# A graph-attention layer on one core: the first group takes h W before the softmax, its attention runs on quarters of the array, and transfers are put in order of use

## The chip, the core and the metric

The kernel runs on one core of a Trainium2 chip. The core has a matrix engine (TensorE, "PE" in the profile, with its weight loads as "PEld"), VectorE (DVE), ScalarE (ACT), GpSimd (POOL) and SyncE (SP), which issues most transfers. ACT and POOL issue transfers too, each from its own queue. The metric is the device time of one execution in microseconds (us); it is the median of three runs. A profiled execution of the same kernel gives the rows that are quoted.

## The reference

Everything is float32. There are 128 graphs of 64 nodes with 512 features. The graph layer has four heads.

```python
h = maximum(layernorm(x), 0)                       # x: [128, 64, 512]
Wh = einsum('bnf,hfo->bhno', h, W_heads)           # four heads, 512 x 512 each
e  = f1[:, :, :, None] + f2[:, :, None, :]         # f1 = Wh . a[:, :512], f2 = Wh . a[:, 512:]
e  = where(adj > 0, leaky_relu(e, 0.01), -1e9)
h1 = elu(einsum('bhnm,bhmo->bhno', softmax(e), Wh))  # heads side by side: [128, 64, 2048]
out = elu(one such head on h1, with W_out (2048 x 512) and a_out)
y  = relu(out @ w1 + b1) @ w2 + b2 + out
return x + layernorm(y) * gamma + beta
```

Two orders are possible for a head: softmax(e) times (h W), or (softmax(e) times h) times W. The scores f1 and f2 need neither product: f1 = h (W a1), so they can be had from h and the "folded" vectors W a1 and W a2.

## The kernel before

**Tiles and groups.** A tile t holds 128 rows, that is two graphs (NB = 2). Four tiles (G = 4) form a group; there are NG = 16 groups. The main loop goes over groups g. In the turn of g it runs `project1(g, h)` for the four heads, then `project2(g)` (the product with W_out), each beside "side" work of other groups: attention weights of later groups (`stage_a`), attention of the second layer (`stage_e(g-1)`), and the feed-forward part of group g-1 (`feed_forward`).

**Large products.** A product of a 512 x 512 block by a group's 512 columns is cut into 2 x 2 blocks and computed with seven block products in place of eight (`unit`). Block products 5, 6, 7 and 4 use sums of weight blocks, which `weight_sums(m)` makes once on GpSimd and stores in DRAM (`TC[m]`); products 1, 2 and 3 use blocks of the weight itself. `piece(m, p)` loads a block (256 KB) on SP's queue into a ring of 11 buffers. For heads 0 and 1 of group 0 the sums are still in SBUF and are used from there (`DIRECT`). Each of the seven is four float32 matmuls of 256 columns, and the profile counts two instructions for one such matmul ("x8").

**First layer of a group.** `norm1(t)` normalizes a tile (statistics on DVE, the power on POOL, the activation on ACT). `transpose_h(t)` turns it on PE, and `project_f(g)` multiplies it by `wa`, the folded vectors. `scores1(g)` sets out the sums f1 + f2, `softmax` (through `attn_weights(p)`, two tiles at a time) makes the weights A on DVE and ACT, `transpose_weights(p)` turns them. `attend1(g)` multiplies the weights with h, before W: four blocks z of all heads, copied out of PSUM by ACT and DVE. `project1(g, h)` then multiplies by W, applies elu, and leaves blocks `H1`, from which `project2(g)` works. So in every group softmax comes first and the large products after it.

**The start.** Before the main loop, the four W_heads are loaded whole on ACT's queue (`fetch`), x, adj and a_heads on SP's. The fold is done for heads 0, 1 and 3 on DVE (`fold_dve`: 8 multiply-and-accumulate instructions per head, against rows of a_heads which `spread_a` spreads over the partitions with PE), for head 2 on PE (`fold_pe`: transposes of W, then matmuls of two columns). Then come `project_f(0)`, `scores1(0)`, the softmax of both tile pairs, the turned weights, `attend1(0)` and `project1(0, 0)`. The weight sums of W_out (`more_sums`, m = 4 to 7) lie beside `project1(0, 1..3)`, behind the softmax's end.

**What sets the order.** The Tile layer puts each engine's instructions in an order by their place in the program, simulated readiness and free buffers; what follows a `high_priority` is drawn forward. Engines then run their own queues in order. A dependency added by hand keeps one instruction behind another. PSUM has six banks for large results (`bank`, tag "mm") and two for small ones (`aux`). SBUF tiles with one tag share a buffer: the W_heads of the start lie in the buffers which later hold h1's blocks (`homes`), their sums in those of the feed-forward part (`stages`).

Of the kernel before, what the change touches and what calls it, by code (L numbers as in the profile page):

```python
# [14 lines left out]
ALPHA = 0.01  # L15
# [7 lines left out]
def gat_preln_kernel(  # L23
# [27 lines left out]

    nc = tc.nc
# [27 lines left out]

    def aux(shape, name):
        return ps.tile(shape, FP, tag="aux", name=name, bufs=2)
# [16 lines left out]
    aj = const.tile([P, N], mybir.dt.int32, name="aj")  # L99
    for b in range(NB):  # L100
        nc.sync.dma_start(out=aj[ts(b, N), :], in_=adj)
# [4 lines left out]
    ah = wk.tile([2 * H * KC, P], FP, tag="elu", name="ah", bufs=3)  # L106
    nc.sync.dma_start(out=ah, in_=a_heads.rearrange("h (r p) -> (h r) p", p=P))
# [9 lines left out]
    def masks():  # L117

        nc.vector.memset(wa, 0.0)
        id32 = const.tile([P, 32], FP, name="id32")  # L120
        nc.vector.tensor_reduce(id32, ident.rearrange("p (j r) -> p r j", r=32), AX.X, ALU.add)
        nc.vector.tensor_add(headrow, id32[:, 0:H], id32[:, H:2 * H])
        nc.vector.tensor_reduce(isf, id32[:, 0:2 * H].rearrange("p (c h) -> p c h", c=2), AX.X, ALU.add)
        for q in range(2):
            par = sm.tile([P, 1], FP, tag="par", name=f"par{q}")
            nc.vector.tensor_reduce(
                par, ident.rearrange("p (a q r) -> p q a r", a=2, q=2)[:, q], AX.XY, ALU.add
            )
            nc.vector.tensor_scalar(isq[:, q], isf, par, None, ALU.mult)
# [3 lines left out]
        nc.vector.tensor_scalar(negm, aj, 0.0, None, ALU.is_gt)  # L133
        nc.vector.tensor_scalar(negm, negm, NEG, -NEG, ALU.mult, ALU.add)
        nc.vector.tensor_add(eye, ident[:, 0:N], ident[:, N:2 * N])
# [6 lines left out]
    homes = ("h11", "h22", "h12", "wh2", "out", "wh2", "out", "wh2", "out", "out")  # L142
    stages = ("ot", "rt", "out", "hS", "ot", "rt", "ot", "rt", "ot", "rt")
    MT, TC = {}, {}
    DIRECT = {}

    def fetch(m):
        MT[m] = big.tile([P, KC, O], FP, tag=homes[m], name=f"pw{m}")
        queue = nc.scalar if m < H else nc.gpsimd
        queue.dma_start(out=MT[m], in_=mats[m].rearrange("(k p) o -> p k o", p=P))  # L150

    def spread_a(m):

        ab = []
        for c in range(2):
            pb = bank(f"pab{m}_{c}").rearrange("p a b -> p (a b)")
            r = 2 * m + c
            nc.tensor.matmul(
                pb, ident[0:2 * H, r:r + 1].to_broadcast([2 * H, P]), ar, start=True, stop=True
            )  # L160
            ab.append(pb)
        return ab

    def turn_a():

        rows = H * 2 * KC
        pt = aux([P, rows], "pah")
        nc.tensor.transpose(pt, ah, ident[0:rows, 0:rows])
        aT = wk.tile([P, H, 2, KC], FP, tag="s1", name="aT")
        nc.scalar.copy(aT.rearrange("p h c o -> p (h c o)"), pt)  # L170
        return aT

    def fold_dve(m, ab):

        for k in range(KC):
            for c in range(2):
                junk = wk.tile([P, O], FP, tag="t", name=f"jk{c}_{m}_{k}")
                nc.vector.scalar_tensor_tensor(
# [4 lines left out]
    def fold_pe(m, aT):  # L183

        pw = aux([P, KC, 2], "pwa")
        for k in range(KC):
            pt = bank(f"pwt{m}_{k}").rearrange("p a b -> p (a b)").rearrange("p (o q) -> p o q", o=KC)
            for o in range(KC):
                nc.tensor.transpose(pt[:, o, :], MT[m][:, k, ts(o, P)], ident)
            wT = wk.tile([P, KC, P], FP, tag="elu", name=f"wT{m}_{k}", bufs=3)  # L190
            nc.scalar.copy(wT, pt)
            for o in range(KC):
                nc.tensor.matmul(
                    pw[:, k, :], wT[:, o, :], aT[:, m, :, o],
                    start=(k == 0 and o == 0), stop=(o == KC - 1), skip_group_check=True,
                )
        nc.scalar.copy(wa[:, :, m:m + H + 1:H], pw)

    def weight_sums(m, after=None):

        w = MT.pop(m)
        b11, b12 = w[:, 0:2, 0:Q], w[:, 0:2, Q:O]
        b21, b22 = w[:, 2:4, 0:Q], w[:, 2:4, Q:O]
        tag = stages[m]
        if tag[1] == "t":
            s = [big.tile([P, 2, 2, Q], FP, tag=f"{tag}{i}", name=f"pt{m}_{i}") for i in range(2)]
        else:
            both = big.tile([P, 2, 2, 2, Q], FP, tag=tag, name=f"pt{m}")
            s = [both[:, 0], both[:, 1]]
# [3 lines left out]
        for ins in free if after is not None else ():  # L213
            tc.add_manual_dep(
                ins.ins, after.ins.name,
                mybir.DependencyInfo(mybir.DependencyClass.Sync, mybir.DependencyReason.DATA),
                reason="the sums come behind it",
            )
# [4 lines left out]
        if m < 2:  # L223
            for p, i in ((5, 0), (6, 1), (7, 2), (4, 3)):
                DIRECT[m, p] = s[i // 2][:, i % 2]

    def piece(m, p):

        if (m, p) in DIRECT:
            return DIRECT.pop((m, p))  # L230
# [109 lines left out]
    def norm_stats(src, tag, t):  # L340
# [4 lines left out]
        if tag == "n1" and t >= 2 * G:  # L345
            tc.add_manual_dep(
                ins.ins, LAST["pe"].ins.name,
                mybir.DependencyInfo(mybir.DependencyClass.Sync, mybir.DependencyReason.DATA),
                reason="x may come late: not in front of what is urgent",
            )  # L350
# [5 lines left out]
        nc.gpsimd.tensor_tensor(rstd, ve, mhalf, ALU.pow)  # L356
        return mv[:, 0:1], rstd

    def norm1(t):
# [7 lines left out]
        if t % G >= 2:  # L367
# [14 lines left out]
    def project_f(g):  # L382


        pf = aux([P, P], f"pf{g}")
        for k in range(KC):
            for j in range(G):
                nc.tensor.matmul(
                    pf[32 * j:32 * j + 32], wa[:, k, :], HT[G * g + j][:, k, :],
                    start=(k == 0), stop=(k == KC - 1), skip_group_check=True,  # L390
                )
        L = sm.tile([P, 2, P], FP, tag="L", name=f"L{g}", bufs=1)
# [12 lines left out]
    def scores1(g):  # L405

        L, R = LR.pop(g)
        pe = [aux([P, 2, H * N], f"s1pe{g}_{a}") for a in range(2)]
        for q in range(2):
            for a in range(2):  # L410
                for b in range(NB):
                    rows, cols = slice(64 * a, 64 * a + 64), slice(b * N, (b + 1) * N)
                    nc.tensor.matmul(
                        pe[a][cols, q, :].rearrange("p (h m) -> p h m", h=H), L[rows, q, cols],
                        R[rows, :, cols], start=(q == 0), stop=True, skip_group_check=True,
                    )
        for a in range(2):
            E1[2 * g + a] = pe[a].rearrange("p t (h m) -> p (t h) m", m=N)

    def softmax(pe, f1, q, tag, t):  # L420
# [4 lines left out]
        mask = negm[:, None, :].to_broadcast([P, q, N])  # L425
        if f1 is None:
            nc.vector.tensor_tensor(e, pe, mask, ALU.add)
        else:
            nc.vector.tensor_tensor(e, pe, f1[:, :, None].to_broadcast([P, q, N]), ALU.add)
            nc.vector.tensor_tensor(e, e, mask, ALU.add)  # L430
        nc.vector.scalar_tensor_tensor(e, e, ALPHA, e, ALU.mult, ALU.max)
        mx = sm.tile([P, q], FP, tag=w + "mx", name=f"{tag}mx{t}")
        nc.vector.tensor_reduce(mx, e, AX.X, ALU.max)
        nc.vector.tensor_tensor(e, e, mx[:, :, None].to_broadcast([P, q, N]), ALU.subtract)
        nc.scalar.activation(e, e, AF.Exp)
        s = sm.tile([P, q], FP, tag=w + "s", name=f"{tag}s{t}")
        nc.vector.tensor_reduce(s, e, AX.X, ALU.add)
        r = sm.tile([P, q], FP, tag=w + "r", name=f"{tag}r{t}")
        nc.vector.reciprocal(r, s)
        if q == 8:  # L440
            A = sm.tile([P, 2, H + 1, N], FP, tag=w + "A", name=f"{tag}A{t}", bufs=1)
            nc.vector.tensor_tensor(
                A[:, :, 0:H], e.rearrange("p (t h) m -> p t h m", h=H),
                r.rearrange("p (t h) -> p t h", h=H)[:, :, :, None].to_broadcast([P, 2, H, N]), ALU.mult,
            )
            LAST["A"] = nc.vector.tensor_copy(A[:, :, H], A[:, :, 0])
# [23 lines left out]
    def transpose_weights(p):  # L470
        A = A1.pop(p)
        for j in range(2):
# [3 lines left out]
            pt = aux([P, NB * H, N], f"s1pt{t}")  # L476
            for h in range(H):
                to = pt[:, h:h + H + 2:H + 1] if h + 1 < H else pt[:, h:h + 2]
                nc.tensor.transpose(to, A[:, j, h:h + 2].rearrange("p b m -> p (b m)"), ident)  # L479
# [87 lines left out]
    def flat(ap):  # L567
        return ap.rearrange("p a b -> p (a b)")

# [3 lines left out]
    def z_sums(g, h):  # L573
        z = ZB[g]
        ZSUM[h] = new_sums(f"z{g}_{h}")
        eng = nc.vector if (g, h) == (0, 0) else nc.gpsimd
        sums(eng, z["S1"][:, h], z["11"][:, h], z["12"][:, h], z["22"][:, h], *ZSUM[h])

    def project1(g, h):
# [3 lines left out]
        first = (g, h) == (0, 0)  # L583
        if h == 0:
            for b in ("11", "12", "S1", "22"):
                tag = "hS" if b == "S1" else "h" + b
                H1[b] = big.tile([P, H, 2, T], FP, tag=tag, name=f"h{b}_{g}")
# [3 lines left out]
        def post(what, a, b=None, to=None):  # L591
# [13 lines left out]
            post, (1, 2, 6, 5, 7, 3, 4) if first else (1, 5, 6, 2, 3, 7, 4),  # L605
# [9 lines left out]
        ]  # L615

# [180 lines left out]
    masks()  # L797
    for t in range(G):
        norm1(t)
    ab = {m: spread_a(m) for m in (0, 1)}  # L800
    aT = turn_a()
    fold_dve(0, ab[0])
    fold_dve(1, ab[1])
    fold_pe(2, aT)
    for t in range(G):
        transpose_h(t)
    fold_dve(3, spread_a(3))
    for m in range(H):
        weight_sums(m, LAST["nb"])
    project_f(0)  # L810
    scores1(0)
    for p in range(2):
        attn_weights(p)
    softmax_end = LAST["A"]
    transpose_weights(0)
    attn = attend1(0)
    for fn in attn[:2]:
        fn()
    head0 = project1(0, 0)
    for fn in head0[:2]:  # L820
        fn()
    transpose_weights(1)
    for fn in attn[2:]:
        fn()
    z_sums(0, 0)
# [14 lines left out]
    def more_sums(m):  # L840
        fetch(m)
        weight_sums(m, softmax_end)

    for t in range(G, 2 * G):
        prefetch(t)
    for g in range(NG):
        if g >= 1:
            side = stage_e(g - 1)
        else:
            side = sum(stage_a(1), [])  # L850
            for i, m in ((5, 4), (9, 5), (12, 6), (17, 7)):
                side.insert(i, lambda m=m: more_sums(m))
        done, n = 0, 6 * H
        for i in range(n):
            if i % 6 == 0:
                steps = head0 if (g, i) == (0, 0) else project1(g, i // 6)
            if (g, i // 2) != (0, 0):
                steps[i % 6]()
            while done * n < (i + 1) * len(side):
# [64 lines left out]
```

## Time and profile before

The three timed runs took 2317.66, 2319.98 and 2321.33 us. The profiled execution has a span of 2318.7 us.

| engine | busy us | share of the span |
|---|---|---|
| PE | 2279.8 | 98% |
| PE weight loads | 1922.7 | 83% |
| DVE | 1272.2 | 55% |
| POOL | 1029.9 | 44% |
| ACT | 905.5 | 39% |

The start by stretches, busy us of each engine:

| stretch, us | PE | DVE | ACT | POOL | transfers, GB/s |
|---|---|---|---|---|---|
| 0 to 60 | 41.38 | 36.37 | 17.32 | 34.84 | 294 |
| 60 to 115 | 54.24 | 35.77 | 30.50 | 38.82 | 168 |
| 115 to 230 | 111.69 | 51.73 | 46.47 | 62.02 | 186 |
| 230 to 370 | 140.00 | 78.34 | 55.90 | 60.41 | 155 |

A row of a group of instructions gives line, engine, operation, the tile written and those read, the shape, and the count. A row of a timeline begins with start and length in us; several alike are merged, and brackets hold the idle time before and what ended it. A row of a wait reads: who waited for whom, then the sum in us, how often, and the longest. A row of a window holds, after its bounds and length, an engine's busy time with its count of instructions, then the clock granted to PE (1.00 is full), the share of transfers and their rate. Matmuls are pipelined: the time from start to start is what one costs, and the length of one is longer.

### The profile page before, as it was taken

The numbers are of one execution on the slowest core, as the hardware profiler recorded it, in microseconds if no ns is written. First come the engines' busy times: TensorE is split into PE (matmuls) and PEld (weight loads), VectorE is DVE, ScalarE is ACT, GpSimd is POOL, SyncE is SP. The second block draws the span as 40 slices with busy tenths as digits, with TensorE's granted clock in tenths as the row PEclk, the third lists the DMA queues.
The fourth block names the chain that finished last, engine by engine and source line by source line (L and its number), as shares of the span: only waits on it lengthen the run. The fifth ranks groups of instructions, "written<-read, shape, count | busy, mean of one in ns | idle before, by whom it ended". The sixth has DMA issues, their size and how long they took to land. (4 is left out here: it accounts for less than half of the span.)

```text
span 2318.7 us, 33446 instructions
## 1 busy us (share of the span) xinstructions
PE 2279.8 (98%) x11933; PEld 1922.7 (83%) x11933; DVE 1272.2 (55%) x2210; ACT 905.5 (39%) x1623; POOL 1029.9 (44%) x917
## 2 busy tenths in 40 slices
PE   6999999999999999999999999999999999999997
PEld 4878888888888888888888888888888888888885
DVE  6635465555646555465555646555464654744427
ACT  2534425153352534425254252533525244251512
POOL 6664544425344352444425444253443525533324
PEclk8999999999999999999999999999999999999999
DMA  8545464554545445454454545445453454635543
GB/s 296 174 171 195 133 183 135 157 161 133 183 135 176 131 147 178 133 182 132 151 171 133 182 135 162 150 140 182 132 179 131 147 180 128 182 119 168 163 146 104
DMA packets 259571, 366.40 MB, mean 158 GB/s; under 512 B 24232, under 2 KB 147144, under 8 KB 259408
## 3 DMA queue, kind: packets, MB, share of 16 engines
q1 hardware_dynamic: 252784, 343.31, 47.3%
q0 software_dynamic: 4512, 16.78, 2.0%
q10 hardware_dynamic: 2112, 4.19, 0.5%
q8 instruction: 96, 1.57, 0.3%
q14 instruction: 67, 0.55, 0.1%
HBM read 336.92 MB, written 27.26 MB: 157 GB/s over the span
## 5 line engine op out<-in xcount | busy, mean ns | idle before, releaser
L322 PE MATMUL g_b<-w,h 128*128 128x256 f32 x2560 | 592.5, 379 | 0.0
L322 PEld LDWEIGHTS g_b<-w,h 128*128 128x128 f32 x2560 | 481.4, 190 | 63.7 <-issue 0.9
L307 PE MATMUL g_a<-z,w 128*128 128x256 f32 x1520 | 360.9, 380 | 0.7 <-DVE g_a L597 0.7
L307 PE MATMUL g_a<-zs_z,w 128*128 128x256 f32 x1504 | 350.9, 381 | 0.0
L307 PEld LDWEIGHTS g_a<-zs_z,w 128*128 128x128 f32 x1504 | 282.0, 190 | 60.8 <-issue 24.3
L307 PEld LDWEIGHTS g_a<-z,w 128*128 128x128 f32 x1520 | 287.2, 190 | 45.0 <-DVE g_a L597 6.1
L601 POOL TENSOR_TENSOR hS<-hS,h 128x512 f32<-128x512 f32 x64 | 83.1, 1299 | 354.8 <-DVE hS L565 354.8
L322 PE MATMUL g_b<-w,hS 128*128 128x256 f32 x1024 | 238.5, 379 | 0.0
L563 ACT ACTIVATE exc<-g_a 128x512 f32<-128x512 f32 x256 | 152.1, 594 | 179.0 <-DVE g_a L597 106.7
L565 DVE SCALAR_TENSOR_TENSOR h<-exc,g_a 128x512 f32<-128x512 f32 x192 | 131.7, 686 | 157.3 <-ACT exc L564 156.2
L322 PEld LDWEIGHTS g_b<-w,hS 128*128 128x128 f32 x1024 | 192.1, 190 | 25.8 <-issue 1.0
L564 ACT ACTIVATE exc<-exc 128x512 f32<-128x512 f32 x256 | 161.5, 631 | 7.0
L631 POOL TENSOR_TENSOR h<-h,h 128x512 f32<-128x512 f32 x64 | 86.8, 1364 | 135.3 <-PE g_b L322 135.3
L631 POOL TENSOR_TENSOR h<-hS,h 128x512 f32<-128x512 f32 x64 | 81.2, 1270 | 142.5 <-PE g_b L322 142.5
L481 ACT COPY at<-s1pt 128x512 f32<-128x512 f32 x64 | 34.7, 588 | 279.8 <-PE s1pt L479 279.8
L332 POOL TENSOR_TENSOR zs_z<-zS,z 128x512 f32<-128x512 f32 x63 | 89.0, 1414 | 122.6 <-PE g_a L307 118.6
L773 POOL TENSOR_TENSOR xr<-xr,bs 128x512 f32<-128x512 f32 x64 | 96.1, 1502 | 72.6 <-DMA xr<-in_x_dram 58.4
L307 PE MATMUL g_c<-ot,w 128*128 128x256 f32 x512 | 122.8, 383 | 1.4 <-DVE ot L735 1.4
L322 PE MATMUL g_d<-w,rt 128*128 128x256 f32 x512 | 121.5, 380 | 2.2 <-DVE o L765 1.5
L307 PE MATMUL g_a<-zS,w 128*128 128x256 f32 x496 | 117.2, 379 | 0.0
L655 DVE SCALAR_TENSOR_TENSOR jf<-wh,ao 128x512 f32<-128x512 f32 x128 | 99.0, 811 | 31.8 <-ACT wh L637 31.6
L333 POOL TENSOR_TENSOR zs_z<-z,zs_z 128x512 f32<-128x512 f32 x63 | 85.1, 1351 | 61.8 <-PE g_a L307 39.1
(159 smaller groups left out, 3485.8 us busy)
## 6 DMA issues: line engine op xcount, KB each, us to landing
w<-tc SPq DMA_DIRECT2D x632, 256.0 KB, 2.7
w<-in_L_gnn_W_heads_dram SPq DMA_DIRECT2D x192, 256.0 KB, 3.0
w<-in_L_gnn_W_out_dram SPq DMA_DIRECT2D x192, 256.0 KB, 2.7
w<-in_L_gnn_w_dram SPq DMA_DIRECT2D x96, 256.0 KB, 2.7
x<-in_x_dram SPq DMA_DIRECT2D x64, 256.0 KB, 3.8
xr<-in_x_dram SPq DMA_DIRECT2D x128, 128.0 KB, 2.7
out_dram<-o SPq DMA_DIRECT2D x128, 128.0 KB, 2.4
tc<-pt POOLq DMA_DIRECT2D x20, 512.0 KB, 4.2
```

Source lines behind the costliest of these rows:

```text
L307: LAST["pe"] = nc.tensor.matmul(bk[:, o, :], w[:, k, ts(o, P)], a[:, k, :], start=start and o == 0 and k == 0, stop=k == 1, skip_group_che ...
L322: LAST["pe"] = nc.tensor.matmul(bk[:, j, :], a[:, k, ts(j, P)], w[:, k, :], start=start and k == 0 and j == 0, stop=i == len(ms) - 1 and k ...
L332: eng.tensor_tensor(s2, s1, a11, ALU.subtract)
L333: eng.tensor_tensor(s4, a12, s2, ALU.subtract)
L481: nc.scalar.copy(AT[t].rearrange("p b h n -> p (b h) n"), pt)
L563: nc.scalar.activation(ex, src, AF.Relu, scale=-1.0)
L564: nc.scalar.activation(ex, ex, AF.Exp, scale=-1.0)
L565: nc.vector.scalar_tensor_tensor(dst, ex, -1.0, src, ALU.add, ALU.max)
L601: nc.gpsimd.tensor_tensor(dst, dst, H1["22"][:, h], ALU.add)
L631: nc.gpsimd.tensor_tensor(dst[:, h], x0[:, h], x1[:, h], ALU.subtract)
L655: nc.vector.scalar_tensor_tensor(junk, WH2[g][:, j], 1.0, ao[:, c, :], ALU.mult, ALU.mult, accum_out=f[:, c, j:j + 1],)
L773: nc.gpsimd.tensor_tensor(xr, xr, bs, ALU.add)
```

## The change

Only group 0 is computed in another way. Its four heads take h W first (`head_w(m, j)`: tile j by head m, four matmuls of 512 columns, the copy by ACT into `HW`). The scores are folded beside it, all four heads on DVE (`fold`); `fold_pe` and `turn_a` go. `attend0(h, r)` then multiplies the turned weights with `HW`, four matmuls of 64 rows and 64 columns of the array for each pair of tiles, and applies elu to the result in its natural layout; `turn0(h, r)` transposes that on PE and copies it into `H1`. `attend1(0)` and `project1(0, h)` are no longer called.

The transfers are put in order: only W of head 0 stays on ACT's queue, heads 1 to 3 go to SP's behind x, adj goes to POOL's, a_heads comes second on SP's, and its other layout `ah` goes. The loads of W_out for `weight_sums` come during the head products, each held behind one of them. The weight sums are all kept in the buffers "ot" and "rt", and `DIRECT` goes, as does `HNS` of group 0. Group 1's transposes and `project_f` lie among group 0's attention, its `scores1`, softmax and turned weights at the beginning of `project2(0)`.

```diff
     X[0] = load(0)
-    aj = const.tile([P, N], mybir.dt.int32, name="aj")
-    for b in range(NB):
-        nc.sync.dma_start(out=aj[ts(b, N), :], in_=adj)
     ar = wk.tile([2 * H, O], FP, tag="elu", name="ar", bufs=3)
...
-    homes = ("h11", "h22", "h12", "wh2", "out", "wh2", "out", "wh2", "out", "out")
+    homes = ("h11", "h22", "h12", "wh2", "out", "hS", "out", "hS", "out", "out")
...
-        queue = nc.scalar if m < H else nc.gpsimd
+        queue = nc.scalar if m == 0 else nc.sync if m < H else nc.gpsimd
...
-        if tag == "n1" and t >= 2 * G:
+        if tag == "n1" and t >= G:
+            behind(ins, LAST["pe"], "x may come late: not in front of what is urgent")
...
-        pf = aux([P, P], f"pf{g}")
+        pf = aux([P, P], f"pf{g}") if g else flat(bank("pf0"))[:, 0:P]
...
+                if g == 0 and k == 0:
+                    behind(ins, LAST["pe"], "the fold is not done sooner")
...
+    def head_w(m, j):
+        pb = aux([P, O], f"hw{m}_{j}")
+        for k in range(KC):
+            LAST["pe"] = LAST["hw", m, j] = nc.tensor.matmul(
+                pb, HT[j][:, k, :], MT[m][:, k, :], start=k == 0, stop=k == KC - 1
+            )
+        nc.scalar.copy(flat(HW[j][:, m]), pb)
+
+    def attend0(h, r):
+        pa = [flat(bank(f"pu{h}_{r}_{b}")) for b in range(NB)]
+        for b in range(NB):
+            rows = slice(b * N, (b + 1) * N)
+            for c in range(2):
+                nc.tensor.matmul(
+                    pa[b][c * N:(c + 1) * N], AT[2 * r + c][rows, b, h, :],
+                    flat(HW[2 * r + c][rows, h]), start=True, stop=True, skip_group_check=True,
+                )
+        for b in range(NB):
+            ex = wk.tile([P, O], FP, tag="elu", name=f"ex0{h}_{r}_{b}", bufs=3)
+            if b == 0:
+                nc.scalar.activation(ex, pa[b], AF.Relu, scale=-1.0)
+                nc.scalar.activation(ex, ex, AF.Exp, scale=-1.0)
+            else:
+                nc.vector.tensor_scalar(ex, pa[b], 0.0, None, ALU.min)
+                nc.scalar.activation(ex, ex, AF.Exp)
+            NAT[h, r, b] = wk.tile([P, O], FP, tag=f"zs{2 + b}", name=f"nat{h}_{r}_{b}")
+            nc.vector.scalar_tensor_tensor(NAT[h, r, b], ex, -1.0, pa[b], ALU.add, ALU.max)
+
+    def turn0(h, r):
+        for b in range(NB):
+            nat = NAT.pop((h, r, b))
+            pt = flat(bank(f"ptu{h}_{r}_{b}")).rearrange("p (c q) -> p c q", c=KC)
+            for c in range(KC):
+                nc.tensor.transpose(pt[:, c, :], nat[:, ts(c, P)], ident)
...
+        if r == 1:
+            nc.gpsimd.tensor_tensor(H1["S1"][:, h], H1["S1"][:, h], H1["22"][:, h], ALU.add)
...
+    for m in range(3):
+        fold(m, ab[m])
+    for j in range(G):
+        transpose_h(j)
+        head_w(0, j)
+    weight_sums(0, LAST["nb"])
+    fold(3, spread_a(3))
+    masks()
+    weight_sums(1, LAST["nb"])
+    for j in range(3):
+        head_w(1, j)
+
+    def more_sums(m):
+        fetch(m, LAST["hw", *{4: (0, 1), 5: (0, 3), 6: (1, 2), 7: (2, 1)}[m]])
+        weight_sums(m)
+
+    more_sums(4)
     project_f(0)
+    weight_sums(2, LAST["nb"])
+    head_w(1, 3)
+    more_sums(5)
+    head_w(2, 0)
     scores1(0)
...
+    transpose_weights(0)
+    head_w(3, 0)
+    attend0(0, 0)
+    attend0(1, 0)
+    head_w(3, 1)
+    transpose_weights(1)
+    turn0(0, 0)
+    attend0(2, 0)
+    head_w(3, 2)
+    turn0(1, 0)
+    attend0(0, 1)
+    head_w(3, 3)
+    turn0(2, 0)
+    attend0(1, 1)
+    turn0(0, 1)
+    attend0(3, 0)
+    turn0(1, 1)
+    attend0(2, 1)
+    for fn in scores[:2]:
+        fn()
+    turn0(3, 0)
+    attend0(3, 1)
+    project_f(1)
+    turn0(2, 1)
+    turn0(3, 1)
...
-            run(project2(g), first + early + norms + scores + turns + [
+            mixed = side1 + attn[:2] + norms[:1] + attn[2:] + norms[1:] + [nothing] * 3
+            run(project2(g), mixed + early + scores + turns + [
                 load_rows, lambda: sums_late(M1), lambda: sums_late(M2)
             ])
```

## The prediction

> **What bounds the kernel now.** I read the page first: the busy row of TensorE (PE) and the table of 40 slices.
>
> ```profile
> PE 2279.8 (98%) x11933; PEld 1922.7 (83%) x11933; DVE 1272.2 (55%) x2210; ACT 905.5 (39%) x1623; POOL 1029.9 (44%) x917
> ...
> PE   6999999999999999999999999999999999999997
> ```
>
> PE is busy in 98% of the span, and only the first and last of the 58 us slices are loose. The diff touches group 0 alone, so the other fifteen groups (140.0 us each in the windows 230 to 370 and 370 to 510) are not at stake: what can change lies before about 185 us, where group 1's first product starts. Second, the waits of PE:
>
> ```profile
> PE pab L158 <- DMA ar<-in_L_gnn_a_heads_dram: 8.2, 1, 8.2
> PE s1pt L479 <- DVE s1A L442: 5.4, 1, 5.4
> PE s1pe L413 <- DVE n1ve L354: 2.8, 1, 2.8
> PE pwt L189 <- DMA pw<-in_L_gnn_W_heads_dram: 2.1, 1, 2.1
> ```
>
> All four stand at the start: 18.5 us in which PE has nothing, because softmax precedes every large product. Third, the timeline of PE (start, length, tile, count):
>
> ```profile
> 22.55 1.09 PE L378 MATMUL pth<-ident,hn 128*128 128x128 f32 x4
> ...
> 35.41 2.15 PE L388 MATMUL pf<-hT,wa 128*32 128x128 f32 x32
> 40.37 1.99 PE L413 MATMUL s1pe<-R,L 64*64 64x256 f32 x16 [2.82 <-DVE n1ve L354]
> 47.74 1.94 PE L479 MATMUL s1pt<-ident,s1A 128*128 128x128 f32 x8 [5.38 <-DVE s1A L442]
> 49.61 6.22 PE L539 MATMUL pz<-at,hn 64*128 64x256 f32 x32
> ...
> 80.51 1.08 PE L388 MATMUL pf<-hT,wa 128*32 128x128 f32 x32
> ...
> 101.84 1.04 PE L479 MATMUL s1pt<-ident,s1A 128*128 128x128 f32 x8
> 102.71 1.89 PE L307 MATMUL g_a<-z,w 128*128 128x256 f32 x8
> ...
> 184.47 1.89 PE L307 MATMUL g_a<-z,w 128*128 128x256 f32 x8
> 186.20 1.89 PE L307 MATMUL g_a<-zS,w 128*128 128x256 f32 x8
> ...
> 218.24 1.09 PE L697 MATMUL pa<-wh,at 64*64 64x512 f32 x8
> 219.26 1.99 PE L307 MATMUL g_a<-zs_z,w 128*128 128x256 f32 x8
> ```
>
> The same 32 score matmuls take 2.15 us at 35 us and 1.08 us at 80 us, the same 8 transposes 1.94 and 1.04: PE runs at half speed until attention's matmuls have streamed for some 4 us. The windows show when it ends:
>
> ```profile
> 44.00:46.00 2.00, 0.00 (x0) 0.50 0.97 375
> ...
> 52.00:54.00 2.00, 2.00 (x13) 0.51 0.33 127
> 54.00:56.00 2.00, 2.00 (x17) 1.00 0.00 0
> ```
>
> (The third number is PE's busy time, the one after the count its clock. Before 41 us the record says 1.00, but the lengths above say one half.) So before 49.6 us no projection work is done, and group 0 is some 50 us late.
>
> [...] 17.5 to 37 us is filled mostly with transposes and two-column matmuls and stays slow. [...]
>
> **The change, part by part.** PE's prices at full clock, from start-to-start times: 8 instructions of 256 columns (four fp32 matmuls, two instructions each) 1.73 us, so one of 512 columns 0.432; 8 transposes 0.87; one attention of four quarter-array matmuls, 512 wide, 1.02 (the shape of L697); the score sets of L388 and L413 1.0 each. At half clock a 512-column instruction of spread_a took 0.853.
>
> Group 0's PE work afterwards, up to its project2:
> - head_w, 16 times four matmuls of 512 columns: 16 x 8 x 0.432 = 55.3. It replaces 28 x 1.73 = 48.4 of the seven-product form: 6.9 more, but it needs only h and W.
> - attend0 8 x 1.02 = 8.2, and turn0's 64 transposes 7.0. attend1(0), which goes, would cost 7.7 warm (as for group 1, 120 to 140 us) and took about 10.
> - transposes of h 1.75, of the weights 1.75, score sets 2.0.
> - spread_a: 12 instructions slow, 10.2, the last four fast, 1.7. The transposed fold of W2 (fold_pe: pwt 3.7 plus pwa 7.0 us busy) goes, as does aT.
> - group 1's transposes and projection of scores, still in this stretch: 2.75.
> Sum 90.7.
>
> It starts when ar lands. ar moves ahead of adj, and three of the 1 MB loads leave ACT's queue for SP's, behind x. x0 landed 2.4 us after its issue ended; with ar's issue ending near 1.8 us I take 5 us (4.2 to 8.2 as bounds). ACT is freed too: it issued loads until 12.2 us and only then normalized; now one load is some 2.9 us of issue, so h of tile 0 is there by 7 to 8, under the 10 us of spread_a. W1 to W3 are needed on PE only every 13.8 us and land by about 20 at the 300 to 365 GB/s seen, so SP's order hides. 5 + 90.7 = 95.7. head_w's first 4 to 5 us run slow: 2.5 more, 98.2.
>
> Fold, masks and softmax now lie beside head_w. DVE needs 32 folds x 0.61 = 19.5, eight tiles' statistics 8, masks 2.5, R and U 1.7, two softmaxes 10.5: 42 of the 60 us before weight transposes are wanted (my sum puts those near 66 us). The fourth head's spread comes about 32 us, its fold ends near 40, scores1 is placed near 54, softmax ends 61 and 66: hidden, with 5 us to spare. head_w's PSUM copies (0.59 us, ACT) hide under 3.46 us each, unless ACT's queue stands behind an exponential that waits for DVE; early on two small PSUM buffers serve both transposes and products. I give these handovers 2 us (0 to 5).
>
> From the first attention on ACT has, per head and half, two activations and one more exponential (3 x 0.6) and two copies (about 0.4 each): 2.6 us, 8 times 21, with head copies 2.4, weight copies 2.3 and group 1's copies 2.4: 28 us, over some 30 us of PE. After the last head_w it is about 15.5 on ACT against 12.4 on PE: 3.5 us of stall (0, if project2's first product, 6.9 us and ready by then, fills it; 8 if every chain is exposed). 98.2 + 2 + 3.5 = 103.7 for project2's start.
>
> project2(0) took 115.68 to 184.47, 68.8 us, with 63.4 of work (48.4, attend1 7.7, group 2's scores 5.5, the late g_a 1.73), so 5.4 of gaps. Now it also holds group 1's scores1 and weight transposes (2.75) and no g_a: 64.4 + 5.4 = 69.8 (gaps 3 to 10: group 1's softmax and group 2's norms come after each other, but the stage has 42 us left after attention). End 173.5 against 184.5: 11.0 us less.
>
> The edits of statistics' order, of the softmax's loop (one piece as before) and of b11/stages have no work of their own. POOL loses hns and z_sums for group 0, and the sums of W_out (four tensor operations of 1.27 and 1.1 of issue, 6.2 each) come earlier: eight sums are 50 us from about 13 us on. The waiting fetches stand in POOL's own queue, ahead of norms and S1 additions. Their waits end with head_w(0,1), (0,3), (1,2), (2,1), near 23, 34, 46 and 58 us; the last load, 7.7 us median to landing, and its sums end near 75. H1's S1 uses that load's buffer and is first written near 90: hidden.
>
> 2318.7 - 11.0 = 2307.7 for the profiled span; the timed runs' median, 2319.98, less 11 gives **2309**.
>
> **The rivals.** (a) *Better packed*: project2's first product fills the turn phase, handovers cost nothing and ar lands at 4.2: 6.3 us more, about 2302. For it: PE has nearly always ready work. Against: two small PSUM buffers. (b) *Gain eaten in attention and turn*: quarter-array attention and transposes alternate for 12.4 us without a large product. If transposes do not hold the clock, this stretch takes 12.4 more, and ACT's 3.5 then hide: 11 - 8.9 = 2 us gain, 2318. With only ACT's 8 exposed, 2313.5. For it: 17 to 37 us above. Against: attention fills half of each 2 us with the whole array. (c) *POOL becomes the bound, slower*: if each fetch of W_out is issued only behind the sums of the one before, a chain of 4 x (7.7 + 6.2) = 56 us follows about 38 us of earlier work and ends near 94; norms behind it push it further. The mechanism decides from the end of the last sum: turn0 of the second half waits for its buffer from 90 on, PSUM banks fill, and PE stops. At 101 the gain is gone; past about 106 the kernel is slower by over 0.2%; an end at 112 gives 2331. For it: POOL waited 4.4 and 10.0 us for W_out's landing at 97 and 121 us. Against: the fetches' waits end long before. (d) The head products could be done early with nothing gained if softmax came no sooner; but PE's slots are then already spent on them, so I give this no share of its own.
>
> **How the numbers follow.** Likeliest 0.52, own range 2304 to 2314. (a) 0.13. (b) 0.25, half of it within 0.2% of before. (c) 0.10. 0.2%, 4.6 us, is about what a measurement of this kernel can tell from no change. Faster (below 2315.3): 0.52 + 0.13 + 0.13 = 0.78; within: 0.12; slower: 0.10. The range runs from 2300 to 2320: it leaves out (c) and little of (a) and (b).
>
> **What would show it.** Right: pab near 5 us; head products from about 15, fast by 20; PE in the first 60 us at 54 or more of busy time instead of 41; group 1's first L307 product near 173. Wrong: PE's waits for ACT copies above 6 us in sum; transposes of turn0 at 0.21 us each instead of 0.11; turn copies released by POOL; project2(0) longer than 75 us.

## The result, and the profile after

The change made the kernel slower. Medians of four runs each, taken together: 2330.4 us (2328.9 to 2332.11) after, 2320.65 (2317.66 to 2321.39) before; the ratio is 1.0045, with a 95% interval of 1.0027 to 1.0062. The forecast was 2309, with a range of 2300 to 2320: wrong in its sign, and outside its range by 10 us. The profiled span is 2329.7 us against 2318.7, 11.0 more.

The page's busy row and PE's row of slices:

```profile
PE 2289.5 (98%) x11856; PEld 1896.2 (81%) x11856; DVE 1274.2 (55%) x2227; ACT 901.9 (39%) x1621; POOL 1014.9 (44%) x908
...
PE   8899999999999999999999999999999999999997
```

The first slice did rise, from 6 to 8: PE has its early work. But the second is an 8 where it was a 9, and PE is busy for 9.7 us more in all, with 77 instructions fewer. PE's waits say where it stands idle now, and its timeline (start, length, tile, count; idle time before and its releaser in brackets) says when:

```profile
PE hw L612 <- ACT hw L615: 7.5, 1, 7.5
PE pab L171 <- POOL n1rs L327: 5.4, 1, 5.4
PE g_a L282 <- ACT t_a L248: 4.0, 1, 4.0
PE pth L351 <- ACT hT L353: 3.2, 2, 2.6
PE s1pt L468 <- DVE s1A L426: 2.6, 2, 2.1
```

```profile
5.36 10.57 PE L171 MATMUL pab<-ar,ident 8*128 8x512 f32 x12 [5.36 <-POOL n1rs L327]
...
18.91 5.46 PE L612 MATMUL hw<-pw,hT 128*128 128x512 f32 x8
...
35.51 14.00 PE L612 MATMUL hw<-pw,hT 128*128 128x512 f32 x32 [0.73 <-ACT hT L353]
...
73.21 5.61 PE L612 MATMUL hw<-pw,hT 128*128 128x512 f32 x8 [7.53 <-ACT hw L615]
...
115.11 1.89 PE L297 MATMUL g_b<-w,h 128*128 128x256 f32 x8
...
125.50 1.43 PE L468 MATMUL s1pt<-ident,s1A 128*128 128x128 f32 x8 [2.10 <-DVE s1A L426]
...
162.22 1.82 PE L351 MATMUL pth<-ident,hn 128*128 128x128 f32 x8 [2.59 <-ACT hT L353]
...
189.35 1.89 PE L282 MATMUL g_a<-z,w 128*128 128x256 f32 x8
...
214.72 3.78 PE L282 MATMUL g_a<-zs_z,w 128*128 128x256 f32 x8 [4.05 <-ACT t_a L248]
```

The old waits for softmax at the start are gone. Two new large ones have come, at 66 and at 211 us. Both cost twice: the products at 73.21 and at 214.72 take 5.61 and 3.78 us instead of 3.60 and 1.89, at a PE clock of 0.50 in both places (72 to 76 and 214 to 220 us), where it was 1.00 before the waits. The windows around the first (the last fields are PE's busy time and count, its clock, the share of transfers and GB/s) show it fall and return:

```profile
70.00:72.00 2.00, 0.00 (x0) 0.56 0.61 177
...
74.00:76.00 2.00, 2.00 (x4) 0.50 0.65 262
...
78.00:80.00 2.00, 2.00 (x12) 1.00 0.53 122
```

So 7.53 us of idling were followed by a clock of 0.50, which was 1.00 again by 78. The prediction counted a slow clock at the start and, in rival (b), for the transposes, but behind no stall.

The difference by stages. Project2(0) starts at 115.11 where 103.7 was forecast (11.4 late), takes 74.24 us where 69.8 was (4.4), and after group 1's first product at 189.35 some 7.0 are lost again around 211 us (4.05 of wait, about 3 of half clock). Of these, 6.1 remain at the end: from that product on the span has 2140.35 us, where before had 2134.23. With the 11.0 of gain that the forecast had: -11.0 + 11.4 + 4.4 + 6.1 = 10.9, against 11.0 measured.

**What holds PE at 66 us.** The timeline of all engines:

```profile
58.94 1.27 POOL L194 TENSOR_TENSOR pt<-pw 128x512 f32<-128x512 f32 x1 [1.19 <-DMA tc<-pt]
...
66.21 1.08 POOL L327 TENSOR_TENSOR n1rs<-n1ve,mhalf 128x1 f32<-128x1 f32 x2
...
68.52 0.50 POOL L337 TENSOR_SCALAR n1nb<-n1mv,n1rs 128x1 f32<-128x1 f32 x2
68.81 0.42 DVE L323 BATCH_NORM_AGGREGATE n1mv<-n1st 128x2 f32<-128x6 f32 x2 [6.54 <-POOL n1nb L337]
68.81 1.52 ACT L339 ACTIVATE hn<-x,n1nb,n1rs 128x512 f32<-128x512 f32 x2 [10.60 <-POOL n1nb L337]
...
69.15 2.87 DVE L420 TENSOR_TENSOR s1e<-s1e,s1mx 128x512 f32<-128x512 f32 x1
...
72.05 0.63 ACT L421 ACTIVATE s1e<-s1e 128x512 f32<-128x512 f32 x1 [1.72 <-DVE s1e L420]
72.59 0.57 ACT L615 COPY hw<-hw 128x512 f32<-128x512 f32 x1
```

Read it from the last row back. The copy that PE waits for is 0.57 us of work, but ACT stands in order behind an exponential (72.05) and two normalizations (68.81). The normalizations waited 10.60 us for group 1's reciprocal deviations and the step after them (n1nb), two operations on a single column per tile, which GpSimd reached only at 66.21: from 58.94 it had the weight sums of the fourth head, with 1.19 us of waiting for its own DRAM write before them. DVE had the variances ready by 59.9. DVE itself then stood for 6.54 us: the statistics of group 1's next two tiles wait for the same n1nb, and the softmax's subtraction (69.15) stands behind them. That subtraction took 2.87 us, and the exponential waited for it; the same instruction takes 0.69 at 76.70, where GpSimd runs no tensor operation. It ends just after the first break between two of GpSimd's operations (71.46 to 71.55). By ACT's row one can divide the stall: its normalizations were over at 70.33, and 1.72 us of waiting for the subtraction followed. An estimate from this is 1.7 us for the long subtraction and the other 5.8 for the queue.

**What holds PE at 211 us** is the long DVE operation alone:

```profile
207.96 5.48 DVE L418 SCALAR_TENSOR_TENSOR s2e<-s2e 128x256 f32<-128x256 f32 x1
...
211.89 1.26 POOL L307 TENSOR_TENSOR zs_z<-zS,z 128x512 f32<-128x512 f32 x1
213.23 1.34 POOL L308 TENSOR_TENSOR zs_z<-z,zs_z 128x512 f32<-128x512 f32 x1
213.36 0.68 DVE L247 TENSOR_TENSOR g_a<-g_a,s_a 128x512 f32<-128x512 f32 x1
...
214.08 0.59 ACT L248 COPY t_a<-g_a 128x512 f32<-128x512 f32 x1 [7.73 <-DVE g_a L247]
```

An operation of group 0's second softmax lies on DVE for 5.48 us and ends just after GpSimd, in tensor operations without a break from 208.22, first has one (213.15 to 213.23); g_a's addition and PE stand behind it. What fills GpSimd's row there are sums of z and h that had been kept back by w2's weight sums, at 202.08 to 207.15. Before, w2's sums ran at 192 to 197 and this softmax at 200.6 to 207.9, its instructions on DVE taking at most 1.67 us, and the one in question:

```profile
203.02 0.41 DVE L431 SCALAR_TENSOR_TENSOR s2e<-s2e 128x256 f32<-128x256 f32 x1
```

The change moved both, and they met.

### The profile page after: what moved, and what is told of

It is laid out like the page before. It is cut to its first block, busy times and chain, and to the rows that moved or that the text cites. A ratio compares the mean times of both kernels' runs of the same rounds, so it can differ in the third digit from the quotient of the medians.

```text
span 2329.7 us, 33260 instructions
## 1 busy us (share of the span) xinstructions
PE 2289.5 (98%) x11856; PEld 1896.2 (81%) x11856; DVE 1274.2 (55%) x2227; ACT 901.9 (39%) x1621; POOL 1014.9 (44%) x908
## 5 line engine op out<-in xcount | busy, mean ns | idle before, releaser
L282 PE MATMUL g_a<-z,w 128*128 128x256 f32 x1440 | 342.8, 381 | 0.0
L282 PE MATMUL g_a<-zs_z,w 128*128 128x256 f32 x1440 | 338.0, 383 | 4.0 <-ACT t_a L248 4.0
L282 PEld LDWEIGHTS g_a<-zs_z,w 128*128 128x128 f32 x1440 | 271.0, 191 | 64.0 <-issue 24.3
L282 PEld LDWEIGHTS g_a<-z,w 128*128 128x128 f32 x1440 | 273.3, 191 | 41.8 <-DVE g_a L586 4.9
L590 POOL TENSOR_TENSOR hS<-hS,h 128x512 f32<-128x512 f32 x60 | 77.9, 1299 | 354.3 <-DVE hS L556 354.3
L554 ACT ACTIVATE exc<-g_a 128x512 f32<-128x512 f32 x240 | 142.7, 594 | 163.4 <-DVE g_a L586 95.6
L556 DVE SCALAR_TENSOR_TENSOR h<-exc,g_a 128x512 f32<-128x512 f32 x180 | 123.6, 686 | 141.9 <-ACT exc L555 141.3
L555 ACT ACTIVATE exc<-exc 128x512 f32<-128x512 f32 x240 | 151.4, 631 | 6.7
L297 PEld LDWEIGHTS g_d<-w,rt 128*128 128x128 f32 x512 | 96.9, 190 | 17.2 <-DVE o L805 2.3
```

Source lines behind the costliest of these rows:

```text
L282: LAST["pe"] = nc.tensor.matmul(bk[:, o, :], w[:, k, ts(o, P)], a[:, k, :], start=start and o == 0 and k == 0, stop=k == 1, skip_group_che ...
L297: LAST["pe"] = nc.tensor.matmul(bk[:, j, :], a[:, k, ts(j, P)], w[:, k, :], start=start and k == 0 and j == 0, stop=i == len(ms) - 1 and k ...
L554: nc.scalar.activation(ex, src, AF.Relu, scale=-1.0)
L555: nc.scalar.activation(ex, ex, AF.Exp, scale=-1.0)
L556: nc.vector.scalar_tensor_tensor(dst, ex, -1.0, src, ALU.add, ALU.max)
L590: nc.gpsimd.tensor_tensor(dst, dst, H1["22"][:, h], ALU.add)
```

## The experiments

Theory 1: what is lost comes from GpSimd, in two ways: small urgent operations stand in its queue behind weight sums, and DVE is held while its operations run without a break. The rivals: ACT is simply too full in the softmax (theory 2), the tie of group 1's normalizations to a head product puts them badly (`t >= G` in place of `2 * G`), or the new order of transfers.

**e1_pool_free**: group 1's norms ahead of head 3's sums in the program, the sums of W_out each held behind the norms that come before them in the program.

```diff
-    weight_sums(3, LAST["nb"])
     norms[0]()
     norms[1]()
+    weight_sums(3, LAST["nb"])
     more_sums(6)
...
     def more_sums(m):
...
-        weight_sums(m)
+        weight_sums(m, LAST["nb"])
```

> Edit: the powers of group 1's norms come before the sums of heads' weights 3 and of W_out 6 and 7 on GpSimd; nothing else. Theory 1 (GpSimd's queue): the 7.5 us for which PE waited at 65.7 us came from those powers standing behind sums, ScalarE's normalization standing behind them, and the copy of a head product behind that. Then the stall and the 1.9 us of half clock after it go, project2(0) starts near 105.5 instead of 115.1 us, and the kernel takes about 2321 us. Theory 2 (softmax): the copy stood behind the exponential, which waits for DVE's softmax; then at least 5 us of the stall stay, and the time falls by under 3 us, to 2327 or more.

2328.76 us, ratio 1.0040 (1.0025 to 1.0055). The wait at 66 us fell from 7.5 to 0.3, so its cause is the order of GpSimd's queue:

```profile
67.40 3.70 PE L612 MATMUL hw<-pw,hT 128*128 128x512 f32 x8 [0.30 <-ACT hw L615]
```

But project2(0) started at 111.52, not 105.5: the sums moved on beside the softmax, and there, in the timeline, a copy of a quarter of a tile takes 6.79 us, to the end of an unbroken row of sums that starts at 76.37:

```profile
75.82 6.79 DVE L431 COPY s1A<-s1A 128x128 f32<-128x128 f32 x1
...
81.27 1.25 POOL L199 TENSOR_TENSOR pt<-pw,pt 128x512 f32<-128x512 f32 x1
```

PE waited there for the turned weights (1.43 us), and one attention behind it took 1.8 us, where 1.02 is usual. The second stall stayed (3.84, now at 207 us). The time is the one that theory 2 gave, not theory 1's 2321; but theory 2 wanted 5 us of the first stall to stay, and it went.

**e2_ffn_sums_later**: only w2's weight sums go, behind group 0's second softmax.

```diff
         A = sm.tile([P, q, NB, N], FP, tag=w + "A", name=f"{tag}A{t}", bufs=1)
-        nc.vector.tensor_tensor(
+        LAST["A2"] = nc.vector.tensor_tensor(
...
-                load_rows, lambda: sums_late(M1), lambda: sums_late(M2)
+                load_rows, lambda: sums_late(M1), lambda: fetch(M2)
...
             side = stage_e(g - 1)
+            if g == 1:
+                side.insert(9, lambda: weight_sums(M2, LAST["A2"]))
```

> Edit: the sums of w2 on GpSimd are held behind group 0's second-layer softmax; nothing else. Theory 1: the 4.05 us stall of PE at 210.7 us and the half clock until 220 come from DVE's score instruction (5.48 us instead of 0.41), which got no turn while GpSimd ran one instruction after the other; moved away, it takes under 1.5 us, and 6 to 7 us go: about 2323.5 us. Theory 2: PE waited there for weight blocks from DRAM or for its own result bank; then the stall stays and the time is within 2 us of 2330.

2325.6 us, ratio 1.0025 (1.0015 to 1.0036). The stall at 211 is gone, and the operation that had taken 5.48 us reads:

```profile
208.16 0.42 DVE L418 SCALAR_TENSOR_TENSOR s2e<-s2e 128x256 f32<-128x256 f32 x1
```

The span is 2324.3, 5.4 less than after's, though group 1's first product came 1.2 later (190.53): 6.6 gained behind it, so that the rest of the kernel takes as long as in before (2133.8 us, and 2134.2). The stall at 66 (7.56) stays, as it should.

**e3_norms_late**: the norms of group 1 behind the third head's products, so that the second half of the queue theory is tried without touching the sums.

```diff
-    norms[0]()
-    norms[1]()
     more_sums(6)
...
         head_w(2, j)
+    norms[0]()
+    norms[1]()
     more_sums(7)
```

> Edit: group 1's norms come after the third head's products in the program, sums on GpSimd as they were. Theory 1: GpSimd is as late as before, but ScalarE's normalizations stand behind the copies that PE needs first, so the stall at 65 us goes; part comes back near 75 to 80 us, when a copy or an exponential stands behind the normalization: 4 to 8 us less, 2322 to 2326. Theory 2 (softmax on DVE and ScalarE holds the copies): the stall stays at 5 us or more, 2327 to 2331.

2334.03 us, ratio 1.0066 (1.005 to 1.0083): slower still, where 2322 to 2326 had been expected. The stall left 66 us and came back at 82, before the first transposes of the attention's result, and eight of these take 1.94 us instead of 1.04:

```profile
86.11 0.81 ACT L339 ACTIVATE hn<-x,n1nb,n1rs 128x512 f32<-128x512 f32 x1 [3.14 <-POOL n1nb L337]
...
89.42 1.94 PE L645 MATMUL ptu<-ident,nat 128*128 128x128 f32 x8 [7.13 <-DVE nat L637]
```

Again a normalization that waits for GpSimd holds ACT (5.67 and 3.14 us), and this time the elu of attend0 is what stands behind it. The stall follows the norms, not the softmax, which speaks against theory 2.

**e4_both**: the edits of e1 and e2 together.

> Edit: e1 and e2 together. If the two stalls are separate, their gains add: 2330.4 - 9.5 - 6.5 = about 2314.5 us, faster than the kernel before by some 6 us. If the second stall only takes up what the first leaves (GpSimd's work is merely moved on), the sum is no better than e1 alone, about 2321.

2320.7 us, ratio 1.0006 (0.9997 to 1.0014), as before the change, and not 2314.5. Against after's 2330.4 it is 9.7 us less, where e1 alone took 1.6 and e2 alone 4.8: no gain eats the other, but e1's is far from the 9.5 that were counted for it. The copy on DVE still takes 6.69 us beside the sums (74.78), PE waits 2.4 us between 80 and 85, and project2(0) starts at 110.38. The next run takes that away.

**e5_pool_off_softmax**: e4, but the last two sums of W_out stand behind the first softmax (the last operation of A), and head 3's behind the last head product.

```diff
     def more_sums(m):
...
-        weight_sums(m)
+        weight_sums(m, LAST["A"] if m > 5 else LAST["nb"])
...
-    weight_sums(3, LAST["nb"])
     norms[0]()
...
     head_w(3, 3)
+    weight_sums(3, LAST["hw", 3, 3])
```

> Edit: e4, and besides the sums of W_out 6 and 7 on GpSimd are held behind the end of group 0's softmax, those of head 3 behind the last head product. In e4 DVE's small copy of the weights (128x128) took 6.69 us instead of 0.23 and PE waited 3.3 us in three pieces between 80 and 85 us, with slower products after. Theory A: [...] with GpSimd off that stretch the copy takes under 0.5 us, the waits go, project2(0) starts near 106.5 instead of 110.4 us, and the time falls by 3 to 4 us, to about 2317. Theory B: the copy waits for readers of its tile or for another engine; then it stays above 3 us and the time within 1.5 us of e4's 2320.7.

2316.32 us, ratio 0.9984 (0.9977 to 0.9991): as theory A had it, and under before. In its timeline GpSimd starts when the softmax is over, and the copy takes 0.23 us:

```profile
73.12 0.23 DVE L431 COPY s1A<-s1A 128x128 f32<-128x128 f32 x1
73.43 1.26 POOL L194 TENSOR_TENSOR pt<-pw 128x512 f32<-128x512 f32 x1 [4.81 <-DVE s1A L431]
```

Project2(0) starts at 106.29, group 1's first product at 178.91. The sums then lie just as densely beside attend0, but DVE's operations there read PSUM (elu's minimum and maximum) and keep their 0.69 us. Nothing of the h W first form was touched between after and this run, and 14.1 us lie between their medians (2330.4 and 2316.32).

**e6_norms_before_sums**: e5, and the z sums of group 1 held behind group 2's norms; group 1's turned weights two steps later in project2(0).

```diff
     def z_sums(g, h):
+        hold = LAST["nb"] if g == 1 and h < 2 else None
...
-        eng.tensor_tensor(s2, s1, a11, ALU.subtract)
+        ins = eng.tensor_tensor(s2, s1, a11, ALU.subtract)
+        if hold is not None:
+            behind(ins, hold, "not in front of the norms")
...
-    side1 = scores[5:] + [nothing] + turns[:4]
+    side1 = scores[5:] + [nothing] * 3 + turns[:4]
```

> Edit: e5, and in project2(0) group 1's z sums on GpSimd come behind group 2's norms, and group 1's weight transposes two steps later in the program. Theory A: the waits of PE in project2(0), 2.1 us for the softmax and 2.6 us for the norms that stand behind z sums in GpSimd's queue, fall below 1 us each, group 1's first product starts near 172 us, and the time is about 2313. Rival: the waits only move on to another place of the stage (attention or the next scores come later by as much); then the time is within 1.5 us of e5.

2313.28 us, ratio 0.9968 (0.9957 to 0.998): 7.2 under before, and the best of all. The 2.6 us wait for hT, which in after had its powers at 158.56, behind z sums from 149.97 on, is gone; group 1's first product comes at 176.55. Project2(0) takes 69.4 us, where e5 took 72.6. The other wait, 2.1 us for s1A, only moved, from 116.69 in e5 to 125.58: that half of the edit took nothing away. So the time came as expected, but not by the expected way: the first product at 172 was not reached. What the second wait hangs on was not tried; in after, where it is the same 2.10 us, the DVE operation that ends it (s1A, 123.57) was itself long, 1.79 us for 0.69.

**e7_transfers_alone**: the kernel before, with nothing but the new order of transfers (a_heads second, adj on POOL's queue, heads 1 to 3 on SP's).

```diff
-    aj = const.tile([P, N], mybir.dt.int32, name="aj")
-    for b in range(NB):
-        nc.sync.dma_start(out=aj[ts(b, N), :], in_=adj)
     ar = wk.tile([2 * H, O], FP, tag="elu", name="ar", bufs=3)
...
-        queue = nc.scalar if m < H else nc.gpsimd
+        queue = nc.scalar if m == 0 else nc.sync if m < H else nc.gpsimd
```

> Edit: the kernel before with the order of the first transfers alone changed (adj on GpSimd's queue, a_heads second on SP's, W of heads 1 to 3 on SP's queue behind x). The spread of a_heads on PE starts near 5.4 instead of 8.2 us in both theories. Theory 1: the softmax chain, which is what group 0 waits for, hangs on the folds, and these on PE's half-speed transposes and on the last W; then little is gained, 0 to 2 us: 2317 to 2319. Theory 2: the start of PE decides: 2.8 us less, about 2316.

2318.61 us, ratio 0.9993 (0.9984 to 1.0001): not to be told from no change. PE starts at 5.43 instead of 8.2, but the softmax's wait of 5.4 us stays; group 1's first product comes at 183.66, 0.8 earlier. By themselves the transfers are neither the loss nor a gain; whether the h W first form needs them was not tried.

**e8_norms_untied**: the change with group 1's statistics no longer tied to a product.

```diff
-        if tag == "n1" and t >= G:
+        if tag == "n1" and t >= 2 * G:
```

> Edit: the changed kernel with one condition undone: group 1's statistics are no longer held behind a head product (t >= 2*G as before, instead of t >= G). Theory 1 (GpSimd's queue): DVE was idle from 31 to 51 us, so the statistics come then, the powers stand further forward in GpSimd's queue, among head 2's sums near 48 us, and ScalarE's normalizations no longer hold the copies at 65 us: that stall of 7.5 us falls below 2 us. GpSimd still runs sums 3, 6 and 7 without a gap beside the softmax, so DVE's long instructions stay, as does the 4 us stall at 210 us: 2322 to 2327. Theory 2: the tie to the head product is harmless and only the softmax's place matters: the stall stays above 5 us and the time within 2 us of 2330.

2331.09 us, ratio 1.0044 (1.0027 to 1.0061): the same as after, and not the 2322 to 2327 of theory 1. The statistics come early now and the power at 48.33, but the step after it (n1nb) only at 55.45, between sums, and the second pair's at 58.28 and 66.53. The stall splits into 2.81 and 1.61 us, less than theory 2 allows and more than theory 1, and project2(0) starts at 114.05, 1.1 us earlier than in after. So the tie isn't the cause; whenever the norms come in this stretch, they come behind sums.

## Why the prediction was wrong

Its steps in their order:

- *PE starts at 5*: right, 5.36.
- *Head products 3.46 us each, the first slow*: right. Four take 14.00 us at 35.51, and the first, at 18.91, 5.46.
- *Quarter-array attention and turn phase*: right. Attention comes every 1.02 us, the transposes at 0.11 each, and the clock stays at 1.00 from 88 to 116. Rival (b) is out.
- *Handovers 2 us (0 to 5)*: the first step that failed. It counted ACT's copy by its 0.59 us and named "an exponential that waits for DVE" as the risk; it did not put the normalizations of group 1 in ACT's queue, nor their statistics in front of the softmax in DVE's, and both wait for GpSimd. Measured: 7.53 us and 1.9 of slow clock in one stall, and 1.5 in two small ones. The risk that it named came true too, for the last 1.7 us of the stall.
- *Eight weight sums on GpSimd, and the waits for W_out, "hidden"*: the second, and the root. The text saw that the fetches stand "ahead of norms and S1 additions" and then asked only when H1's S1 buffer would be needed, at 90 us. The norms were the earlier customer, by over 20 us. A chain of eight sums, 50 us in one queue, was costed at nothing without asking when the norms behind it are wanted.
- *The stages edit has no work of its own*: so it has not, but with only "ot" and "rt" a sum must wait for the DRAM write of the one before; 1.19 and 1.10 us of GpSimd's time at 58 and 61.
- *Softmax on DVE ends at 61 and 66*: failed, 74.6 and 80.7. It stood 6.54 us behind the statistics that wait for GpSimd, and its instructions were counted at their undisturbed length; beside dense sums one took 2.87 instead of 0.69. The profile of before has such a case: at 104.91 an operation of the softmax on 128x512 (s1A) lies on DVE for 5.19 us, beside GpSimd's sums. It cost PE nothing there, and the prediction did not use it.
- *Project2(0) 69.8 us (gaps 3 to 10 of the 5.4)*: 74.24, gaps 9.8. The range held it, the value didn't; a power behind GpSimd's sums made most of the excess: without that, e6 takes 69.4. About 1.6 of it depends on the run: after the wait of 2.59 us the clock was 0.60 at 162 to 164 and eight transposes took 1.82 us, while in e4 and e5 the same wait stood (2.58 and 2.59), the transposes behind it took 1.14, and the stage took 72.6; e5's mean clock from 115 to 185 was 1.00.
- *Nothing is at stake behind 185 us*: failed by 6.1 us. A changed start moved w2's sums on top of group 0's second softmax (e2).

Rival (c) had the engine that decides, and its sign, at 0.10, but another place and mechanism. The last sums did end late, at 91.2 where the likeliest case had 75 and this rival 94, but before the 101 from which it saw a loss, and no S1 buffer was waited for. Its 2331 for an end at 112 lies near the measured 2330.4 by luck. Of the signs of being wrong, the one that came was PE's waits for ACT copies above 6 us.

That the gain itself is real, e5 and e6 show: with GpSimd's work laid elsewhere, project2(0) starts at 106.29 and 107.19, within 2.6 and 3.5 us of the forecast's 103.7, and the medians lie 4.2 and 7.2 us under before's of the same session, of the 11.0 forecast. The edits of e2 and e6 were not tried on the kernel before; PE's waits for normalizations sum to 1.8 us there, and no stall like that at 211 is in it, so by an estimate they would give it about 2 us. How the stall at 66 us divides between GpSimd's queue and its hold on DVE is read from one trace; e1 moves norms and sums together. Left as it is in every run is the half-speed start up to about 22 us (in after, twelve instructions of `spread_a` take 10.57 us at 5.36, and two of the same shape 1.12 at 24.73). It differs from run to run: the first head product takes 5.28 to 6.70 us where 3.60 is usual, so a start that is 1 us earlier or later tells nothing.

## What to carry to other kernels

When work on an in-order engine is drawn forward, list every small operation that then stands behind it and ask who waits for that one first; one-column operations of a normalization, kept back behind weight sums, stopped the matrix engine for 7.5 us here, most of it by their place in the queue. A stall on PE of the 4 and 7.5 us seen here also cost a clock of 0.50 behind it (about 3 and 1.9 us), so it was dearer than its length. A new schedule at the start can make two things meet 100 us later: gains and losses behind the edited stretch belong in the range.

## What the hardware showed that was not expected

GpSimd's operations can hold one of DVE's over several of theirs that follow each other without a break: 6.79 and 6.69 us for a 128x128 copy of 0.23, 5.48 for a 128x256 operation of 0.42, 2.87 for one of 0.69. With GpSimd's work moved away the first took 0.23 (e5) and the second 0.42 (e2). Each ended 0.1 to 0.6 us after the row of GpSimd's tensor operations first broke off, while GpSimd's own lengthened little (1.60 and 1.71 us where DVE was let in, for 1.27). It isn't a strict rule: in e1 two operations of DVE (69.45 and 71.27) came through between two sums that followed each other directly, in 1.06 and 0.92 us, and what decides this is open. Transfers are not the cause: in e1 none ran from 80 to 82 us, and the copy was held all the same. By what way GpSimd holds DVE is not shown. Of the kinds, the runs show that the copy and the operations with two SBUF operands were held, that those that read PSUM were not (0.69 us, e5), nor was a reduction with one operand at 61.60, 0.67 us, while a sum ran from 61.31.
